# Two of 128 row tiles per history position fetched by SyncE, one DMA per row, instead of by GpSimd gathers

## The chip, the cores and the metric

The kernel runs on one NeuronCore of a Trainium2 chip. The metric is the device time of one execution in microseconds; the median of several executions is given. The engines are called by the names of the profile: PE (TensorE), DVE (VectorE), ACT (ScalarE), POOL (GpSimd) and SP (SyncE). SP computes nothing: it issues DMAs.

## The reference

It is the deep-interest network of a recommender, in float32, for a batch B of 16384 and L = 200 history positions, with embeddings of D = 64 numbers and a table of V = 100000 items. Cut to what matters:

```python
it = i_emb[item]                       # [B, 64]
h = i_emb[hist]                        # [200, B, 64]: 3,276,800 rows of the table
feat = concat([h, it, h - it, h * it], axis=-1)
a = dice(feat @ au_W1 + au_b1, au_alpha, axis=1)   # 36 hidden units; moments over B for each l
w = a @ au_W2 + au_b2
cur = sum(w * h, axis=0)
z = concat([u_emb[user], it, c_emb[cate], cur], axis=-1)
# then two dense layers with dice, and a last dense layer: [B, outputs]
```

`dice(x, alpha)` is `x * (p + alpha * (1 - p))` with `p = sigmoid((x - mean) / sqrt(var + eps))`. The indices of hist are random over the whole table.

## The kernel before, in words

**Preparation.** A table in HBM is built first, with 128 numbers (512 bytes) a row: the item's embedding and, behind it, the part of the hidden layer that depends on that embedding alone. So one fetched row brings both. The tensor `xi` in HBM holds the part that depends on `it` alone.

**Tiling.** The batch is cut into NT = 128 tiles of P = 128 rows. TD = 16 tiles make one chunk of 2048 rows, and there are ND = 8 chunks. A step k is one chunk of one position: l = k // 8, c = k % 8; there are 1600 steps. The loop `For_i` (L381) unrolls LPB = 10 positions, 80 steps, and runs 20 times; at the end of each pass all engines meet at a barrier.

**One step** (L344) does, with a software pipeline over k:
- `fetch(k)` (L295): POOL issues 16 indirect DMAs (`gather`, L138; the instruction has line L141), each of 128 rows of 512 bytes, by one column of `idx`, into `land[k % 4]`; SP loads `xi[c]` into `xit[k % 2]` (L298).
- ACT copies `xit` of k-1 into PSUM `px` (L353).
- DVE accumulates for k-11: `pw` times the embedding (L357), added to `curT` (L360).
- `turn(k-1)` (L300): DVE transposes the landed rows into `hx[(k-1) % 10]`, in four instructions, each of 64 partitions by 1024 elements (L306). ACT copies the embedding half into PSUM `pg` (L367).
- `hidden(k-2)` (L315): DVE adds `px` to the hidden half (L319) and takes its moments (L321). `product(k-1)` (L310): DVE multiplies by the item (L312), and PE adds the product's matmul to `px` (L179).
- For k-10 ACT and DVE apply the dice gate (L364, L374, L375), and PE multiplies by the second weight into `pw` (L179).

**Order.** Each engine works through its own queue in the order in which the code names the instructions (`manual_schedule`). At the first step of each l, ahead of everything else of the step, `load_hist_ids` (L151, the DMA has line L152) loads the indices of l+1 into `idx[(l+1) % 2]`; the same buffer served l-1, so SP holds that load until the last gather of l-1 has landed. SP holds the load of `xit` of step k until ACT has copied the one of step k-2, which ACT does in its step k-1. POOL holds the first gather of step k until the turn of step k-4 has freed `land`. Waits on SP's DMAs use eight semaphores in turn, so a DMA of SP waits for the one eight before it. POOL's gathers do likewise.

Of the kernel before, what the change touches and what calls it, by code (L numbers as in the profile page):

```python
# [8 lines left out]
F32 = mybir.dt.float32  # L9
I32 = mybir.dt.int32  # L10
# [4 lines left out]
P = 128  # L15
D = 64
EPS = 1e-8
CH = 512
S = 32
CD = 2 * CH  # L20
LPB = 10
LAND = 4
IDX = 2
XI = 2
RING = 10


@with_exitstack
def din_kernel(
# [24 lines left out]
    nc = tc.nc  # L54
    L, B = r_hist.shape
    NT = B // P
    TD = 2 * CD // P
    ND = NT // TD
    V = i_emb.shape[0]
# [3 lines left out]
    const = ctx.enter_context(tc.tile_pool(name="const", bufs=1))  # L63
# [7 lines left out]
    def quarter(e, g, n=S):  # L71

        return slice((2 * e + g) * S, (2 * e + g) * S + n)
# [21 lines left out]
    for e in range(2):  # L95
        rows = au_W1.rearrange("(g d) a -> d g a", d=D)[e * S : (e + 1) * S]
        for g in range(2):
            r = quarter(e, g)
            nc.sync.dma_start(au_w[r], rows)
            for q, (a0, n) in enumerate(parts):  # L100
                c, a = quarter(q, g, n), slice(a0, a0 + n)
# [6 lines left out]
    for g in range(2):  # L108
        for q, (a0, n) in enumerate(parts):
            r, a = quarter(q, g, n), slice(a0, a0 + n)  # L110
# [12 lines left out]

    land = [const.tile([P, TD, 2 * D], F32, name=f"land{i}") for i in range(LAND)]
    idx = [const.tile([P, NT], I32, name=f"idx{i}") for i in range(IDX)]
    stats = [const.tile([P, 2 * ND, nc.vector.BN_STATS_DIM], F32, name=f"st{i}") for i in range(2)]
    rstds = [const.tile([P, 1], F32, name=f"rs{i}") for i in range(2)]
    shifts = [const.tile([P, 1], F32, name=f"sh{i}") for i in range(2)]
# [5 lines left out]
    table = dram.tile([V, 2 * D], F32, name="table")  # L134
# [3 lines left out]
    def gather(dst, ids, rows):  # L138

        for n in range(ids.shape[1]):  # L140
            nc.gpsimd.indirect_dma_start(  # L141
                out=dst[:, n, :],
                out_offset=None,
                in_=rows,
                in_offset=bass.IndirectOffsetOnAxis(ap=ids[:, n : n + 1], axis=0),
            )
# [2 lines left out]
        nc.sync.dma_start(t, ids.rearrange("(p n) -> p n", n=NT))  # L149

    def load_hist_ids(i, l):  # L151
        nc.sync.dma_start(idx[i], r_hist[ds(l, 1), :].rearrange("l (p n) -> p (l n)", n=NT))  # L152

    def by_tile(t, i):

# [41 lines left out]
    with ExitStack() as start:  # L197
        pre = start.enter_context(tc.tile_pool(name="pre", bufs=3))
        ids = [start.enter_context(tc.tile_pool(name=f"ids{i}", bufs=1)).tile(
            [P, NT], I32, name=f"ids{i}") for i in range(3)]  # L200
        for t, v in zip(ids, (r_item, r_user, r_cate)):
            load_ids(t, v)
        load_hist_ids(0, 0)

        per = V // P
# [69 lines left out]
    with ExitStack() as main:  # L275
        ring = main.enter_context(tc.tile_pool(name="ring", bufs=1))
        hx = [ring.tile([P, 2, CD], F32, name=f"hx{i}") for i in range(RING)]
        xit = [ring.tile([P, CD], F32, name=f"xit{i}") for i in range(XI)]
        hm = ring.tile([P, CD], F32, name="hm")
        gate = ring.tile([P, CD], F32, name="gate")  # L280


        for t in hx + [pw, land[-1 % LAND]]:
            nc.vector.memset(t, 0.0)

        for t in px:
            layer(t, [(blk_m, hx[0][:, 0])])
        for i in range(2):
            for c in range(2 * ND):
                nc.vector.bn_stats(stats[i][:, c, :], hx[0][:, 0, :CH])  # L290
            nc.vector.memset(rstds[i], 0.0)
            nc.vector.memset(shifts[i], 0.0)
        nc.sync.dma_start(xit[-1 % XI], xi[ND - 1])

        def fetch(k):  # L295
            l, c = divmod(k, ND)
            gather(land[k % LAND], idx[l % IDX][:, ts(c, TD)], table)
            nc.sync.dma_start(xit[k % XI], xi[c])  # L298

        def turn(k):  # L300

            rows = land[k % LAND].rearrange("p n (s e c) -> p n s e c", s=2, e=2)
            for i in range(2):
                for e in range(2):
                    dst = hx[k % RING][ts(e, D), :, ts(i, CH)]
                    nc.vector.transpose(  # L306
                        dst.rearrange("p s (n t) -> p n s t", t=S), rows[ts(i, D), :, :, e]
                    )

        def product(k):  # L310

            nc.vector.tensor_mul(hm, pg, itT[:, k % ND])  # L312
            layer(px[k % 2], [(blk_m, hm)], onto=True)

        def hidden(k):  # L315

            l, c = divmod(k, ND)
            x = hx[k % RING][:, 1]
            nc.vector.tensor_add(x, px[k % 2], x)  # L319
            for i in range(2):  # L320
                nc.vector.bn_stats(stats[l % 2][:, 2 * c + i, :], x[:, ts(i, CH)])  # L321

        def moments(l):

            i = l % 2
            mv = small.tile([P, 2], F32, tag="mv", name="mv")
            nc.vector.bn_aggr(mv, stats[i].rearrange("p c s -> p (c s)"))
            other = small.tile([P, 2], F32, tag="other", name="other")
            for q in range(2):
                for g in range(2):  # L330
                    nc.vector.tensor_copy(other[quarter(q, g)], mv[quarter(q, 1 - g)])  # L331
            total = small.tile([P, 2], F32, tag="total", name="total")
            nc.vector.tensor_add(total, mv, other)
            mean = small.tile([P, 1], F32, tag="mean", name="mean")
            nc.vector.tensor_scalar_mul(mean, total[:, 0:1], 0.5)
            dev = small.tile([P, 1], F32, tag="dev", name="dev")
            nc.vector.tensor_sub(dev, mv[:, 0:1], mean)
            half = small.tile([P, 1], F32, tag="half", name="half")
            nc.vector.tensor_scalar_mul(half, total[:, 1:2], 0.5)
            var = small.tile([P, 1], F32, tag="var", name="var")  # L340
            nc.vector.scalar_tensor_tensor(var, dev, dev, half, ALU.mult, ALU.add)  # L341
            scale_and_shift(mean, var, P, rstds[i], shifts[i])

        def step(k, first=None, last=None):  # L344


            def has(j):
                return (first is None or j >= first) and (last is None or j <= last)

            if has(k):  # L350
                fetch(k)
            if has(k - 1):
                nc.scalar.copy(px[(k - 1) % 2], xit[(k - 1) % XI])  # L353
            if has(k - 11):

                j = k - 11
                nc.vector.scalar_tensor_tensor(  # L357
                    pw, pw, au_bias2, hx[j % RING][:, 0], ALU.add, ALU.mult
                )
                nc.vector.tensor_add(curT[:, j % ND], pw, curT[:, j % ND])  # L360
            if has(k - 10):
                j = k - 10
                i, x = j // ND % 2, hx[j % RING][:, 1]
                nc.scalar.activation(gate, x, AF.Sigmoid, bias=shifts[i], scale=rstds[i])  # L364
            if has(k - 1):
                turn(k - 1)
                nc.scalar.copy(pg, hx[(k - 1) % RING][:, 0])  # L367
            if has(k - 2):
                hidden(k - 2)
            if has(k - 1):  # L370
                product(k - 1)
            if has(k - 10):

                nc.scalar.activation(pg, gate, AF.Identity, bias=au_al, scale=au_1al)  # L374
                nc.vector.tensor_mul(x, pg, x)  # L375
                layer(pw, [(w2_rep, x)])
            if has(k - 2) and (k - 2) % ND == ND - 1:
                moments((k - 2) // ND)

        steps = LPB * ND  # L380
        with tc.For_i(0, L, LPB) as l0:  # L381
            with tc.manual_schedule():
                for k in range(steps):
                    if k % ND == 0:
                        l = k // ND + 1
                        load_hist_ids(l % IDX, (l0 + l) if l < LPB else (l0 + l) % L)
                    step(k)
        with tc.manual_schedule():
            for k in range(steps, steps + 11):
                step(k, first=0, last=steps - 1)  # L390


    with ExitStack() as head:
# [5 lines left out]
        for g in range(2):  # L399
            t = fin.tile([P, 4, Z1], F32, name=f"w1{g}")  # L400
            nc.vector.memset(t, 0.0)
            for e in range(2):
                rows = W1.rearrange("(f d) z -> d f z", d=D)[e * S : (e + 1) * S]
# [13 lines left out]
        for i, (v, n) in enumerate(((alpha1, Z1), (alpha2, Z2))):  # L417
            t = fin.tile([n, 1], F32, name=f"al{i}")
# [17 lines left out]
        for c in range(ND):  # L436
            rows = land[c % LAND].rearrange("p (s n) d -> p s (n d)", s=2)
# [20 lines left out]
        for m in range(2 * ND):  # L458
            a = work.tile([Z1, CD], F32, tag="a1", name="a1")
# [6 lines left out]
        for c in range(ND):  # L466
            a = work.tile([Z2, TD, 2, 2, S], F32, tag="a2", name="a2")
            for g in range(2):
                p, zm = (
                    t.rearrange("z (i n t) -> z i n t", i=2, t=S)  # L470
                    for t in dice(1, Z2, 2 * c + g, rstd, shift)
                )
# [38 lines left out]
```

## Time and profile before

| | us |
|---|---|
| median of 3 runs | 36814.77 (36811.52 to 36815.77) |
| the profiled execution | 32902.92 |
| its span, first to last instruction | 32901.1 |
| POOL, DVE, PE, ACT busy | 24515.6, 20753.5, 9945.4, 7691.1 |
| gathers of the loop (L141) | 25600, 943 ns each |
| transposes of the loop (L306) | 6404, 1239 ns each |
| first gather of the loop starts at | 489.46 |

The runs take 11.9% longer than the profiled execution; within each kind, the numbers agree closely. The profile's spans, waits and durations are all of the profiled execution. A group's row gives its line in the code, the engine, the operation, what it writes and reads, the count, the busy time, the mean duration of one in ns, and the idle time of the engine just before these instructions with what ended most of it; "issue" means that the engine waited for nothing that the profile shows. SPq is the queue of SP.

### The profile page before, as it was taken

Reading aid. Unit: us, or ns where it says so; the run is one execution under the profiler, and the core shown is the slowest. Engines: PE = TensorE matmul, PEld = TensorE weight load, DVE = VectorE, ACT = ScalarE, POOL = GpSimd, SP = SyncE. Lnnn points to the kernel's source line nnn. Section 1 sums busy time; section 2 is a strip of 40 time slices with the busy share of each in tenths; the row PEclk is TensorE's granted clock in tenths of the full one; section 3 lists DMA queues with packets and bytes.
Section 4 is the critical chain, followed back from the end, with each engine's and each line's share of the span. In section 5 each row is a group of like instructions: output and inputs, shape, how many; then the busy total and the mean of one; then the engine's idle time right before and its main releaser. Section 6 shows DMA issues by size and latency. Waiting matters only on the chain. (4 is left out here: it accounts for less than half of the span.)

```text
span 32901.1 us, 97527 instructions
## 1 busy us (share of the span) xinstructions
PE 9945.4 (30%) x13656; PEld 3845.6 (12%) x13656; DVE 20753.5 (63%) x20780; ACT 7691.1 (23%) x7146; POOL 24515.6 (75%) x25988
## 2 busy tenths in 40 slices
PE   3222222222222222222222222222322222222234
PEld 1111111111111111111111111111111111111112
DVE  7666666666666666666666666666666666666665
ACT  1222222222222222222222222222222222222222
POOL 7777777777777777777777777777777777777774
PEclk6666666666666666666666666666666666666666
DMA  5222222222222222222222222222222222222221
GB/s 158 79 79 80 79 79 78 79 80 79 79 79 79 79 78 81 78 80 79 79 79 79 80 79 79 79 79 79 79 78 81 79 79 79 79 79 79 80 79 53
DMA packets 1208018, 2647.92 MB, mean 80 GB/s; under 512 B 549094, under 2 KB 575366, under 8 KB 1201286
## 3 DMA queue, kind: packets, MB, share of 16 engines
q0 software_dynamic: 831488, 1691.97, 19.6%
q1 hardware_dynamic: 365382, 887.25, 8.7%
q10 hardware_dynamic: 10560, 63.79, 0.5%
q14 instruction: 576, 4.72, 0.0%
q8 instruction: 12, 0.20, 0.0%
HBM read 2577.30 MB, written 63.91 MB: 80 GB/s over the span
## 5 line engine op out<-in xcount | busy, mean ns | idle before, releaser
L141 POOL DMA_INDIRECT land<-table,idx x25600 | 24153.0, 943 | 7882.1 <-issue 7715.6
L179 PE MATMUL px<-hm,blk_m 128*128 128x512 f32 x6404 | 5971.8, 1088 | 22551.3 <-DVE hm L312 22551.3
L306 DVE STREAM_TRANSPOSE hx<-land 64x1024 f32<-64x1024 f32 x6404 | 7936.4, 1239 | 4282.0 <-DMA land<-table,idx 4217.2
L367 ACT COPY pg<-hx 128x1024 f32<-128x1024 f32 x1601 | 1627.5, 1017 | 19460.1 <-DVE hx L306 19460.1
L357 DVE SCALAR_TENSOR_TENSOR pw<-pw,au_bias,hx 128x1024 f32<-128x1024 f32 x1611 | 2082.6, 1293 | 5223.7 <-PE pw L179 5009.3
L179 PEld LDWEIGHTS px<-hm,blk_m 128*128 128x128 f32 x6404 | 1879.6, 324 | 25581.8 <-DVE hm L312 23927.8
L179 PE MATMUL pw<-hx,w_rep 128*128 128x512 f32 x6440 | 3869.3, 732 | 37.1 <-DVE hx L375 37.1
L375 DVE TENSOR_TENSOR hx<-pg,hx 128x1024 f32<-128x1024 f32 x1610 | 1971.8, 1225 | 2044.2 <-ACT pg L374 2044.2
L374 ACT ACTIVATE pg<-gate,au_al,au_1al 128x1024 f32<-128x1024 f32 x1610 | 1943.5, 1207 | 4330.1 <-DVE hm L312 4299.7
L179 PEld LDWEIGHTS pw<-hx,w_rep 128*128 128x128 f32 x6440 | 1800.6, 280 | 2851.0 <-issue 1973.4
L321 DVE BATCH_NORM_STATS2 st<-hx 128x6 f32<-128x512 f32 x3204 | 2061.1, 685 | 55.1
L360 DVE TENSOR_TENSOR curT<-pw,curT 128x1024 f32<-128x1024 f32 x1611 | 1972.6, 1224 | 54.9
L319 DVE TENSOR_TENSOR hx<-px,hx 128x1024 f32<-128x1024 f32 x1602 | 1962.0, 1225 | 49.5
L364 ACT ACTIVATE gate<-hx,sh,rs 128x1024 f32<-128x1024 f32 x1610 | 1991.9, 1237 | 3.1
L312 DVE TENSOR_TENSOR hm<-pg,itT 128x1024 f32<-128x1024 f32 x1601 | 1931.6, 1206 | 0.0
L353 ACT COPY px<-xit 128x1024 f32<-128x1024 f32 x1601 | 1594.8, 996 | 1.9 <-PE px L179 1.7
L364 ACT ACT_TABLE_LOAD x222 | 284.8, 1283 | 4.5 <-DVE sh L193 0.5
L188 ACT ACT_TABLE_LOAD x203 | 260.4, 1283 | 3.8
L179 PE MATMUL px<-rT,blk_h 128*128 128x512 f32 (+1 forms) x196 | 163.9, 978 | 226.2 <-DVE rT L162 226.2
L188 ACT ACTIVATE std<-var,eps 128x1 f32<-128x1 f32 x201 | 59.2, 295 | 456.0 <-DVE var L341 456.0
L331 DVE COPY other<-mv 32x2 f32<-32x2 f32 x804 | 155.2, 193 | 15.1
L353 ACT ACT_TABLE_LOAD x21 | 26.9, 1283 | 567.0 <-DMA idx<-in_r_hist 321.1
(74 smaller groups left out, 1754.0 us busy)
## 6 DMA issues: line engine op xcount, KB each, us to landing
xit<-xi SPq DMA_DIRECT2D x1601, 512.0 KB, 3.7
land<-table,idx POOLq DMA_INDIRECT x25600
table<-tab ACTq DMA_DIRECT2D x48, 1024.0 KB, 4.2
tab<-in_L_rec_i_emb SPq DMA_DIRECT2D x48, 512.0 KB, 4.4
idx<-in_r_hist SPq DMA_DIRECT2D x201, 64.0 KB, 1.8
ucT<-t ACTq DMA_DIRECT2D x16, 512.0 KB, 2.7
land<-ucT SPq DMA_DIRECT2D x16, 512.0 KB, 4.2
xi<-t ACTq DMA_DIRECT2D x8, 512.0 KB, 2.9
```

What stands on the lines that cost most here:

```text
L141: nc.gpsimd.indirect_dma_start(out=dst[:, n, :], out_offset=None, in_=rows, in_offset=bass.IndirectOffsetOnAxis(ap=ids[:, n : n + 1], axis=0),
L179: nc.tensor.matmul(dst[:, cols], lhsT, rhs[:, cols], start=(j == 0 and not onto), stop=(j == len(pairs) - 1), skip_group_check=onto,)
L306: nc.vector.transpose(dst.rearrange("p s (n t) -> p n s t", t=S), rows[ts(i, D), :, :, e])
L312: nc.vector.tensor_mul(hm, pg, itT[:, k % ND])
L319: nc.vector.tensor_add(x, px[k % 2], x)
L321: nc.vector.bn_stats(stats[l % 2][:, 2 * c + i, :], x[:, ts(i, CH)])
L357: nc.vector.scalar_tensor_tensor(pw, pw, au_bias2, hx[j % RING][:, 0], ALU.add, ALU.mult)
L360: nc.vector.tensor_add(curT[:, j % ND], pw, curT[:, j % ND])
L364: nc.scalar.activation(gate, x, AF.Sigmoid, bias=shifts[i], scale=rstds[i])
L367: nc.scalar.copy(pg, hx[(k - 1) % RING][:, 0])
L374: nc.scalar.activation(pg, gate, AF.Identity, bias=au_al, scale=au_1al)
L375: nc.vector.tensor_mul(x, pg, x)
```

## The change

In each l, two of the 128 tiles, the last of chunk 3 and the last of chunk 7, are no longer gathered by POOL. SP fetches their 256 rows, each with a DMA of its own from a byte address that it holds in a register, into one of four tiles `side` of [128, 128]. Each step issues 32 such rows, a quarter of a tile, behind its load of `xit`; they belong to the tile that is turned four to seven steps later. The addresses come from a second load per l of the indices concerned, into `addr` (256 numbers in one partition), which DVE multiplies by 512, the bytes of a row; one instruction of SP then loads 32 of them into 32 registers. The first tile's 128 rows are fetched ahead of the loop. The turn of chunk 3 and of chunk 7 becomes eight transposes: four of 64 x 960 from `land`, four of 64 x 64 from `side`.

```diff
+NS = 2
+SIDE = 4
+ROW = 4 * 2 * D
+    side = [const.tile([P, 2 * D], F32, name=f"side{i}") for i in range(SIDE)]
+    addr = [const.tile([1, NS * P], I32, name=f"addr{i}") for i in range(IDX)]
...
     def load_hist_ids(i, l):
-        nc.sync.dma_start(idx[i], r_hist[ds(l, 1), :].rearrange("l (p n) -> p (l n)", n=NT))
+        ids = r_hist[ds(l, 1), :]
+        nc.sync.dma_start(idx[i], ids.rearrange("l (p n) -> p (l n)", n=NT))
+        t = addr[i]
+        with nc.allow_non_contiguous_dma(reason="one index of each partition"):
+            nc.sync.dma_start(
+                t.rearrange("o (c p) -> o c p", c=NS),
+                ids.rearrange("l (p c n) -> l c n p", c=NS, p=P)[:, :, NT // NS - 1],
+            )
+        nc.vector.tensor_scalar_mul(t, t, ROW)
+
+    def has_side(k):
+        return (k + 1) % (ND // NS) == 0
...
+        flat = table.rearrange("v d -> (v d)").bitcast(U8)
+
+        def rows_by_address(m, part, of):
+
+            l, c = divmod(m, NS)
+            dst = side[m % SIDE].bitcast(U8)
+            n = P // of
+            _, at = nc.values_load_multi_w_load_instructions(
+                addr[l % IDX][:, c * P + part * n : c * P + (part + 1) * n],
+                engines=(mybir.EngineType.SP,), min_val=0, max_val=ROW * (V - 1),
+                skip_runtime_bounds_check_because="the DMA checks the address against the table",
+            )
+            for j, a in enumerate(at):
+                p = part * n + j
+                nc.sync.dma_start(dst[p : p + 1], flat[ds(a, ROW)].rearrange("(o d) -> o d", o=1))
 
         def fetch(k):
             l, c = divmod(k, ND)
-            gather(land[k % LAND], idx[l % IDX][:, ts(c, TD)], table)
+            n = TD - has_side(k)
+            gather(land[k % LAND][:, :n], idx[l % IDX][:, c * TD : c * TD + n], table)
             nc.sync.dma_start(xit[k % XI], xi[c])
+            m, part = divmod(k, ND // NS)
+            rows_by_address(m + 1, part, ND // NS)
 
         def turn(k):
 
-            rows = land[k % LAND].rearrange("p n (s e c) -> p n s e c", s=2, e=2)
-            for i in range(2):
-                for e in range(2):
-                    dst = hx[k % RING][ts(e, D), :, ts(i, CH)]
-                    nc.vector.transpose(
-                        dst.rearrange("p s (n t) -> p n s t", t=S), rows[ts(i, D), :, :, e]
-                    )
+            n = TD - has_side(k)
+            tiles = [(slice(0, n), land[k % LAND][:, :n])]
+            if has_side(k):
+                tiles.append((slice(n, TD), side[k // (ND // NS) % SIDE].unsqueeze(1)))
+            for at, rows in tiles:
+                rows = rows.rearrange("p n (s e c) -> p n s e c", s=2, e=2)
+                for i in range(2):
+                    for e in range(2):
+                        dst = hx[k % RING][ts(e, D), :, ts(i, CH)]
+                        nc.vector.transpose(
+                            dst.rearrange("p s (n t) -> p n s t", t=S)[:, at],
+                            rows[ts(i, D), :, :, e],
+                        )
...
+        for part in range(ND // NS):
+            rows_by_address(0, part, ND // NS)
         steps = LPB * ND
         with tc.For_i(0, L, LPB) as l0:
```

More of the change, by code (lines that the diff above doesn't have):

```diff
@@ L25 @@
 RING = 10
+NS = 2
+SIDE = 4
+ROW = 4 * 2 * D
+U8 = mybir.dt.uint8
 @with_exitstack
@@ L284, in din_kernel @@
             nc.vector.memset(t, 0.0)
+        for t in side:
+            nc.vector.memset(t, 0.0)
         for t in px:
```

## The prediction

> **What bounds the kernel now.** I read the busy line of the page, the costliest groups, the timeline of one step in mid-loop, the waits of SyncE's queue, then the instructions of single lines. First the page's busy line and three groups (line, engine, operation, count, busy us, mean ns, idle before and its releaser):
>
> ```profile
> PE 9945.4 (30%) x13656; PEld 3845.6 (12%) x13656; DVE 20753.5 (63%) x20780; ACT 7691.1 (23%) x7146; POOL 24515.6 (75%) x25988
> L141 POOL DMA_INDIRECT land<-table,idx x25600 | 24153.0, 943 | 7882.1 <-issue 7715.6
> L306 DVE STREAM_TRANSPOSE hx<-land 64x1024 f32<-64x1024 f32 x6404 | 7936.4, 1239 | 4282.0 <-DMA land<-table,idx 4217.2
> xit<-xi SPq DMA_DIRECT2D x1601, 512.0 KB, 3.7
> ```
>
> POOL is 75% busy, yet it is the bound: of its 7882 us of idle time before gathers, 7716 are "issue", time in which it waited for nothing. Gathers follow each other at a fixed pitch; DVE is what waits, 4217 us in all for rows to land. The timeline of one step (start, us, engine, operation, idle before):
>
> ```profile
> 15070.12 0.95 POOL L141 DMA_INDIRECT land<-table,idx  x1 [0.30 <-issue]
> 15070.17 5.00 DVE L306 STREAM_TRANSPOSE hx<-land 64x1024 f32<-64x1024 f32 x4 [2.87 <-DMA land<-table,idx]
> 15070.19 0.34 SPq L152 DMA_DIRECT2D idx<-in_r_hist  x1
> ...
> 15090.09 0.94 POOL L141 DMA_INDIRECT land<-table,idx  x1 [0.30 <-issue]
> 15090.30 5.00 DVE L306 STREAM_TRANSPOSE hx<-land 64x1024 f32<-64x1024 f32 x4 [2.83 <-DMA land<-table,idx]
> ```
>
> Sixteen gathers lie between the two POOL rows: 19.97 us, 1.248 us each (0.94 of work, 0.30 of issue). 25600 of these are 31959 us of the 32901 us span. DVE's idle time ahead of its transposes, 2.7 us a step (4217/1563), is its whole slack: every other idle stretch of its step is a dependence on PE or ACT. SP now does two things a step, and mostly waits; its queue's waits (us, times, longest), and its DMA instructions (duration ns min/median/max):
>
> ```profile
> SPq L298 <- ACT px L353: 20885.5, 1222, 45.0
> SPq L152 <- DMA land<-table,idx: 8655.8, 720, 45.1
> L152 SPq DMA_DIRECT2D idx<-in_r_hist x201: 342/343/430, 9.2 to 32366.2; - x101
> L298 SPq DMA_DIRECT2D xit<-xi x1600: 319/320/596, 498.3 to 32476.9; - x178
> DMA to landing us min/median/max: 1.7/1.8/2.0
> 4.03 0.42 SPq L113 DMA_DIRECT2D au_w<-in_L_rec_au_W  x1
> 4.49 0.37 SPq L111 DMA_DIRECT2D au_bias<-in_L_rec_au_b  x1
> 4.90 0.25 SPq L112 DMA_DIRECT2D au_al<-in_L_rec_au_alpha  x1
> 5.20 0.30 SPq L113 DMA_DIRECT2D au_w<-in_L_rec_au_W  x1
> ```
>
> The load of idx has its address in a register and holds SP for 0.343 us; back to back at the program's start, a DMA takes 0.25 to 0.43 us with 0.04 to 0.05 between two. The landing row is that of idx.
>
> [...] both queues together hold the DMA engines for 28% of the span (19.6 and 8.7), so issuing time is the thing to save. [...]
>
> **The change, part by part.** The timed runs (median 36814.77) lie 11.9% above the profiled execution (32902.92, its span and 1.8 us around it). No view says why. The sums are made against 32902.92 and carried over by ratio; if the whole excess sits in the 25984 gathers, each costs 0.151 us more there, 1.40 us, which gives nearly the same.
>
> (a) Removed: two of 128 gathers per l, 400 in all, on the engine that sets the end: 400 x 1.248 = 499 us less.
>
> (b) Added on SP, in every step: one register load of 32 words and 32 row DMAs, between two xit loads. A row at the idx row's 0.343 plus 0.045 is 0.39; 32 are 12.5 us (9.6 at 0.25+0.05, 15.4 at 0.43+0.05). The register load is in no view. [...] I take 4.0, an estimate[...]. With the xit load (0.42) a step of SP is 16.9 us, between 10.6 and 22.2. SP is further held at the idx load of each l until the gathers of the l before have landed (the 8656 us above), so it cannot bank time across an l: it needs 8 x 16.9 + 1.5 for idx and addr + 2.5 for the landing = 139 us, while POOL takes 126 x 1.248 = 157.3. Hidden, with 18 us to spare; it decides from 19.2 us a step ((157.3 - 4)/8). Behind SP's rows stands the next xit load: ACT's copy into px waits for that, and through PE and DVE all else does.
>
> (c) Waits of the rows. In the built program each DMA of SP waits for the one eight before it to land. At 1.8 us (the idx load) eight in flight allow one per 0.23 us; this is nothing until a row takes 8 x 0.39 = 3.1 us. The xit load's 3.7 us is covered, since a register load and seven rows follow it.
>
> (d) addr on DVE. Once per l DVE gets the multiply by 512 (1 x 256, 0.15 to 0.35 us; the 128x1 multiplies take 0.147 to 0.154) at the head of step 8l, where it waits for the addr load. That DMA stands behind the idx load, so behind the same landing that releases the turn; I estimate it lands 4 to 12 us later (idx took 1.8; 256 small descriptors add to it). Queued behind the multiply are the two accumulations and then the turn, so the turn is late by 7 to 15 us. POOL notices only when the turn of step k-4 is missing, about three steps or 53 us of cover; DVE wins back 2.3 us a step (2.7 less the 0.3 by which POOL's mean step shrinks), 18 us per l. Cost: nothing, and at a loop boundary nothing either, as DVE is idle there for 14.3 us.
>
> (e) Turns. A side step has eight transposes for four. The 64x512 form takes 0.71 and the 64x1024 form 1.24, so 0.18 fixed and 1.04 ns an element: 4 x (1.18 + 0.25 - 1.24) = 0.8 us, 1.6 per l, within the same slack.
>
> (f) Start. Before the loop SP fetches the first 128 rows. It gets going at about 497 us, needs 124 x 0.39 + 3 x 4 = 60, and only then issues idx, addr and xit of step 0. DVE, held by the first addr, does its first turn near 590, while POOL wants that buffer after 63 gathers, 489.5 + 78.6 = 568. A stall of some 23 us, once[...].
>
> Sum: 32902.9 - 499 + 23 = 32427, 0.9855 of before. On the timed runs 36815 x 0.9855 = 36281; I take 36,285. If the excess over the profile is not in the gathers, 36815 - 476 = 36,340; own range 36,230 to 36,420.
>
> **Rivals.** *SP becomes the bound.* One mechanism: a row DMA plus its share of the register load costs more than 0.59 us ((19.2 - 0.42)/32; about 0.66 if POOL's pitch is 1.40 in the timed runs). [...] Against it: 0.343 us in the trace for a DMA with an address in a register. At the upper ends (22.2 us a step) an l takes 8 x 22.2 + 4 = 181.6, the loop 36320 against 32036, and the whole, with 164 us of loop boundaries, 37,374; if SP is slower in the timed runs as POOL may be, more. I give 37,400.
>
> *DVE becomes the bound through addr.* If the 256 descriptors land late enough (turn late by more than about 18 us), DVE no longer catches up within an l, and the rest is paid 200 times: at 30 us late 200 x 12 = 2400 less the 499, some 38,700. Against it: the idx load of 64 KB lands in 1.8 us.
>
> *No difference.* In the timed runs something other than POOL sets the pace (the excess of 11.9% is unexplained), with room for (b) and (d): 36,815. Against it: no engine but POOL is within 2 us of its step in the profile.
>
> That the rows are not where the diff puts them is excluded: the built program has 32 row DMAs after each xit load and 126 gathers per l.
>
> **How the numbers follow.** Forecast 0.60; SP bound 0.26; DVE bound 0.08; no difference 0.06. What a measurement of this kernel can tell from no change is about 0.2%, 74 us. Faster 0.60, same 0.06, slower 0.34. Low end 36,200: 400 gathers at 1.40 are 560 us, no start stall, and little beyond. The high end must take in most of the SP case, from its 37,374 part of the way to the same scaled by 1.119 (41,800): 38,400 leaves out about 0.12 above.
>
> **What would show it.** Right: 25200 gathers at 0.94 with 0.30 of issue before them; SP waiting for ACT's px copy in most steps; the gap before the gathers at one place near 568 us only; the multiply waiting for addr once per l, and turns back on their landing before the l ends. Wrong: gathers idle for DVE's turn throughout, ACT's px copy waiting for the xit DMA, a register load near or above 6 us, row DMAs above 0.43 us or with waits between them; or turns waiting for the multiply in every step.

## The result, and the profile after

The changed kernel took 45896.81 us (median of 4 runs, 45853.32 to 45938.01), the kernel before beside it 36813.14 (4 runs, 36807.65 to 36815.77): 1.2468 times as long, interval 1.2446 to 1.2489. The forecast was 36285.

That is half of the result. The experiments ran in six batches, each with the kernel before beside it. In the first batch it took 36839 us, as in the runs above; in the five later ones it took 32901 to 32903 us, the time of the profiled execution that the forecast was worked from (32902.92). There the same changed kernel took 32514.80 us (4 runs, 32513.69 to 32515.51): 0.9882 of before, interval 0.9866 to 0.9899, faster by 387 us. The two settings are called S (before 36.8 ms) and F (before 32.9 ms) below. Nothing in this study chooses between them, and what they are is not known: the batches were put on chips with several numbers, and one number occurs in both. So there are two profiles after.

First setting S. The page of the changed kernel: the busy line, and the rows that answer to those shown of before (line, engine, operation, count | busy us, mean ns | idle before and its releaser).

```profile
PE 9890.8 (22%) x13656; PEld 3823.3 (8%) x13656; DVE 21020.5 (46%) x22589; ACT 7686.2 (17%) x7146; POOL 24137.3 (53%) x25588
L148 POOL DMA_INDIRECT land<-table,idx x25200 | 23774.7, 943 | 21182.4 <-DVE hx L349 12331.0
L349 DVE STREAM_TRANSPOSE hx<-land 64x1024 f32<-64x1024 f32 (+1 forms) x6404 | 7813.7, 1220 | 106.5 <-DMA land<-table,idx 36.6
L397 ACT COPY px<-xit 128x1024 f32<-128x1024 f32 x1601 | 1620.5, 1012 | 26407.9 <-DMA xit<-xi 25251.3
L167 DVE TENSOR_SCALAR addr<-addr 1x256 int32<-1x256 int32 x201 | 57.7, 287 | 5471.7 <-DMA addr<-in_r_hist 5471.7
```

POOL is busy for 53% of the span and waits 12331 us for DVE's turns. ACT waits 25251 us for the `xit` load, a row that the forecast named as the mark of being wrong. In the profile of before, the same copy waited for 2 us in all:

```profile
L353 ACT COPY px<-xit 128x1024 f32<-128x1024 f32 x1601 | 1594.8, 996 | 1.9 <-PE px L179 1.7
```

`xit` stands behind the rows in SP's queue, and SP itself waits for almost nothing; among its waits (us, times, longest) the largest at the line of the rows is

```profile
SPq L328 <- DMA side<-table: 355.7, 545, 1.9
```

The trace of S lacks many semaphore records (it holds 167,944 updates, that of F 569,179), so a view of waits can miss some; the starts and durations of all 51,328 row DMAs are in it. SP's instructions at the row line and at the register load (count: ns min/median/max, first and last start in us):

```profile
L328 SPq MOVE side<-table x51328: 1/29/1413, 594.0 to 45560.5; - x200
L328 SPq DMA_DIRECT2D side<-table x51328: 1/228/1419, 594.1 to 45560.6; - x200
L321 SPq TENSOR_LOAD <-addr x1604: 2/2057/3800, 576.3 to 45548.3; - x179
```

So SP is the bound. From one idx load to the next is 224.5 us in the mean, 28.1 us a step, and 200 of these are 44,900 of the 45,936 us span. The medians are below what was forecast; it is the maxima that count. SP's timeline shows when (start, us, count):

```profile
20020.20 35.70 SPq L328 DMA_DIRECT2D side<-table  x14
20058.00 0.70 SPq L334 DMA_DIRECT2D xit<-xi  x1
20064.31 17.54 SPq L328 DMA_DIRECT2D side<-table  x32
...
20107.13 20.32 SPq L328 DMA_DIRECT2D side<-table  x32
20128.26 0.00 SPq L334 DMA_DIRECT2D xit<-xi  x1
20130.13 25.18 SPq L328 DMA_DIRECT2D side<-table  x32
...
20181.03 10.68 SPq L328 DMA_DIRECT2D side<-table  x32
```

The same 32 rows take 10.7 us or 25, and once the last 14 of a step take 36. In the slow stretches a MOVE is as slow as a row DMA, in the mean 1.12 us from its start to the next. Sorted by how long POOL has been gathering without a stop (stops over 1 us), or has been stopped, the mean time from the start of such an instruction to that of SP's next one is, worked out from the trace of 5 to 45 ms:

```
ns                      MOVE   row DMA
POOL gathering  < 4 us    85      277
               4-12 us   246      353
                >12 us  1119     1122
POOL stopped    < 3 us   549      512
               3-10 us   176      331
                >10 us    67      270
```

A row (one MOVE, one DMA) costs 0.34 us beside a POOL that stopped a while ago and 2.24 us late in a run of gathers. (The 0.36 and 2.28 of an expectation below count SP's other DMAs and its waits in.) Half of the rows go out while POOL is stopped, a third in the first 12 us of a run of gathers; the remaining 18% take 18 of the 40 ms. POOL in turn stops because SP is late: it waits the 12331 us for DVE's turns, which come behind the 25251 us that ACT waits for `xit`. The mean of the loop is 0.77 us a row.

Now setting F. The same rows of the changed kernel's page there:

```profile
PE 9909.3 (30%) x13656; PEld 3837.2 (12%) x13656; DVE 21024.2 (65%) x22589; ACT 7692.9 (24%) x7146; POOL 24139.3 (74%) x25588
L148 POOL DMA_INDIRECT land<-table,idx x25200 | 23776.7, 944 | 7872.6 <-issue 7536.4
L349 DVE STREAM_TRANSPOSE hx<-land 64x1024 f32<-64x1024 f32 (+1 forms) x6404 | 7823.1, 1222 | 2004.7 <-DMA land<-table,idx 1936.7
L167 DVE TENSOR_SCALAR addr<-addr 1x256 int32<-1x256 int32 x201 | 68.8, 342 | 2454.7 <-DMA addr<-in_r_hist 2454.7
L397 ACT COPY px<-xit 128x1024 f32<-128x1024 f32 x1601 | 1595.6, 997 | 5.2 <-PE px L197 3.9
```

POOL is the bound as before, and its idle time is "issue" again. ACT's copy waits 5 us in all. SP's waits, its instructions, and its timeline there:

```profile
SPq L160 <- DMA land<-table,idx: 6109.8, 419, 34.6
SPq L334 <- ACT px L397: 3018.6, 605, 7.5
```

```profile
L321 SPq TENSOR_LOAD <-addr x1604: 2023/2062/3908, 462.2 to 32092.9; - x179
L328 SPq MOVE side<-table x51328: 29/29/38, 480.2 to 32105.1; - x200
L328 SPq DMA_DIRECT2D side<-table x51328: 224/228/407, 480.3 to 32105.1; - x200
```

```profile
20118.90 0.90 SPq L334 DMA_DIRECT2D xit<-xi  x1
20122.09 10.32 SPq L328 DMA_DIRECT2D side<-table  x32
20132.50 0.36 SPq L334 DMA_DIRECT2D xit<-xi  x1
20135.07 10.73 SPq L328 DMA_DIRECT2D side<-table  x32
```

No MOVE is longer than 38 ns. A step of SP, from one `xit` load to the next, takes 13.0 to 13.6 us where it doesn't wait, and SP waits for ACT and for landings of gathers, not ACT for it.

### The profile page after: what moved, and what is told of

It is laid out like the page before. It is cut to its first block, busy times and chain, and to the rows that moved or that the text cites. A ratio compares the mean times of both kernels' runs of the same rounds, so it can differ in the third digit from the quotient of the medians.

```text
span 45936.2 us, 207379 instructions
## 1 busy us (share of the span) xinstructions
PE 9890.8 (22%) x13656; PEld 3823.3 (8%) x13656; DVE 21020.5 (46%) x22589; ACT 7686.2 (17%) x7146; POOL 24137.3 (53%) x25588
## 3 DMA queue, kind: packets, MB, share of 16 engines
q0 software_dynamic: 818688, 1665.73, 13.9%
## 5 line engine op out<-in xcount | busy, mean ns | idle before, releaser
L148 POOL DMA_INDIRECT land<-table,idx x25200 | 23774.7, 943 | 21182.4 <-DVE hx L349 12331.0
L349 DVE STREAM_TRANSPOSE hx<-land 64x1024 f32<-64x1024 f32 (+1 forms) x6404 | 7813.7, 1220 | 106.5 <-DMA land<-table,idx 36.6
L167 DVE TENSOR_SCALAR addr<-addr 1x256 int32<-1x256 int32 x201 | 57.7, 287 | 5471.7 <-DMA addr<-in_r_hist 5471.7
L349 DVE STREAM_TRANSPOSE hx<-side 64x64 f32<-64x64 f32 x1604 | 383.9, 239 | 35.0
L188 DVE STREAM_TRANSPOSE tab<-px 64x512 f32<-64x512 f32 (+1 forms) x196 | 139.6, 712 | 138.6 <-issue 96.8
```

The costliest lines, as they stand in the source:

```text
L148: nc.gpsimd.indirect_dma_start(out=dst[:, n, :], out_offset=None, in_=rows, in_offset=bass.IndirectOffsetOnAxis(ap=ids[:, n : n + 1], axis=0),
L349: nc.vector.transpose(dst.rearrange("p s (n t) -> p n s t", t=S)[:, at], rows[ts(i, D), :, :, e],)
```

## The experiments

The first batch met setting S, all later ones F. Theory A, after the first profile: SP's instructions slow down while POOL gathers. B: rows and register loads are too dear by themselves. C: the addr load holds SP. In the diffs `-` and `+` are against the changed kernel where nothing else is said.

**1. The kernel before again** (`b_again`, no edit), for a second profile of it.

> The kernel before, unchanged, profiled beside the others. If the profile of before was taken under other conditions than its timed runs, this one spans about 36,810 us and shows where the 3,910 us lie: longer gathers (1.40 us a gather), or idle time of POOL. If the profiler itself makes the difference, it spans 32,900 again and nothing of the excess can be seen.

36838.59 us against 36839.44, ratio 1.0 (0.999 to 1.0009). Its page holds the other half of the puzzle:

```profile
L141 POOL DMA_INDIRECT land<-table,idx x25600 | 26449.6, 1033 | 9454.1 <-issue 8588.3
L357 DVE SCALAR_TENSOR_TENSOR pw<-pw,au_bias,hx 128x1024 f32<-128x1024 f32 x1611 | 2082.8, 1293 | 13185.9 <-remote 10157.2
L306 DVE STREAM_TRANSPOSE hx<-land 64x1024 f32<-64x1024 f32 x6404 | 7922.0, 1237 | 296.4 <-DMA land<-table,idx 227.0
```

In the profile of before, gathers took 943 ns and DVE waited 4282 us at its turns. Here gathers take 1033 ns and follow each other at 1.40 us, both in the mean ((26449.6 + 9454.1)/25600; the median pitch is 1.254), and DVE no longer waits for landings but 13186 us ahead of L357, for PE's result in `pw`. In the first profile of before that wait was

```profile
L357 DVE SCALAR_TENSOR_TENSOR pw<-pw,au_bias,hx 128x1024 f32<-128x1024 f32 x1611 | 2082.6, 1293 | 5223.7 <-PE pw L179 5009.3
```

So the 11.9% between that profile and the timed runs was a difference of setting. Not every step between engines is slower in S. Worked out from the two traces, DVE to PE, DVE to ACT and ACT to DVE take the same 0.03 to 0.06 us in both, in the median; but from the end of PE's last matmul into `pw`, as the profile models that end, to DVE's start on it is 0.04 us in the first profile and 5.2 here. One step in S:

```profile
20024.00 2.81 PE L179 MATMUL pw<-hx,w_rep 128*128 128x512 f32 x4
20031.62 1.29 DVE L357 SCALAR_TENSOR_TENSOR pw<-pw,au_bias,hx 128x1024 f32<-128x1024 f32 x1 [8.74 <-remote]
```

**2. The POOL half alone.** No rows, no register loads, no addr; the side tiles stay zero.

```diff
-            nc.sync.dma_start(
-                t.rearrange("o (c p) -> o c p", c=NS),
-                ids.rearrange("l (p c n) -> l c n p", c=NS, p=P)[:, :, NT // NS - 1],
-            )
-        nc.vector.tensor_scalar_mul(t, t, ROW)
...
-            rows_by_address(m + 1, part, ND // NS)
...
-            rows_by_address(0, part, ND // NS)
```

> The half of the change on POOL alone: 126 gathers per l, the side tiles left at zero, no row DMAs, no register loads, no addr (two tiles per l of the result are left out). If POOL's gathers set the pace in the timed runs as in the profile: 36,813 less 400 x 1.25 to 1.40, so 36,250 to 36,315. If something else sets the pace there: 36,813.

> The kernel of pool_part (126 gathers per l; no rows, register loads or addr, so the side tiles stay zero). Where the kernel before takes 32.9 ms: the forecast says that all that SP and DVE are given to do costs no more than the 23 us of its start stall, so 32490 to 32515 us, and the changed kernel's 32515 lies 0 to 25 us above it. If the 100 us lost at the pass ends come from SP's longer program: 32400 to 32430 us. Where it takes 36.8 ms: 36410 us again.

In S 36409.66 us, 0.9883 of before (0.9866 to 0.9899), 430 us less. In F 32498.95, 0.9877 (0.9861 to 0.9894), 403 less. So the loss in S is wholly in what SP and DVE were given, and in F all of that together costs 16 us (32515 less 32499). The page in F:

```profile
L148 POOL DMA_INDIRECT land<-table,idx x25200 | 23776.3, 944 | 7858.5 <-issue 7709.1
L340 DVE STREAM_TRANSPOSE hx<-land 64x1024 f32<-64x1024 f32 (+1 forms) x6404 | 7829.5, 1223 | 3506.9 <-DMA land<-table,idx 3442.2
```

**3. No gathers in the loop**: nothing but the 256 rows per l is fetched.

```diff
-        for t in hx + [pw, land[-1 % LAND]]:
+        for t in hx + [pw] + land:
...
-            gather(land[k % LAND][:, :n], idx[l % IDX][:, c * TD : c * TD + n], table)
```

> The changed kernel without the loop's gathers (the rows of land stay zero, so the result leaves them out); SP's rows, register loads and addr as in the change. Theory A (SP's instructions slow down while POOL gathers): a row takes its undisturbed 0.32 us throughout, SP needs 13 us a step, and DVE sets the pace at 17 to 18 us a step, 28,000 to 30,000 us in all. Theory B (SP's rows and register loads are too dear by themselves): SP keeps its 28 us a step, about 45,500 us. Theory C (the addr load alone holds SP, some 80 us per l): 200 x (13 x 8 + 80) = 36,800 and 870 more, about 37,700 us.

> The kernel of no_gathers (the gathers of the loop are left out, so nothing but the 256 rows per l is fetched), which took 28452 us on the chip where the kernel before takes 36.8 ms. Theory A3 (the two kinds of chip differ only in what runs beside gathers): where the kernel before takes 32.9 ms it takes the same, 28350 to 28550 us. Rival (the chip of the first runs is slower in everything): 25400 to 27500 us.

28452.58 us in S (0.7723 of before, 0.7708 to 0.7739), 28360.88 in F (0.862, 0.8606 to 0.8634). SP's row line in S, beside a POOL that does nothing in the loop:

```profile
L328 SPq MOVE side<-table x51328: 29/29/38, 590.5 to 28059.2; - x200
L328 SPq DMA_DIRECT2D side<-table x51328: 224/228/432, 590.6 to 28059.2; - x200
```

All 51328 rows at the pace of setting F; this settles A against B. In F these rows run from 480.0 to 27961.7 us. From the first row to the last it is thus 27469 us in S and 27482 in F, equal to 0.05%. The rows start 110 us later in S; so the 92 us between the medians lie ahead of the loop, where POOL gathers too. The two settings differ beside gathers and nowhere else that this kernel shows. With the gathers go their packets (818,688 in the queue `software_dynamic` of the changed kernel, 12,288 here) and, in F, most semaphore updates (14.4 per us in the kernel before, 5.67 here); this run takes all of them away together.

**4. addr loaded once**, ahead of the loop (later rows are those of the first positions).

```diff
-    def load_hist_ids(i, l):
+    def load_hist_ids(i, l, first=False):
...
+        if not first:
+            return
         t = addr[i]
...
-        load_hist_ids(0, 0)
+        load_hist_ids(1, 1, True)
+        load_hist_ids(0, 0, True)
```

> The changed kernel with addr loaded ahead of the loop alone, so the 256 rows of an l are those of l = 0 or 1 (the result leaves the right rows of these tiles out); the rows, register loads and gathers are all there. Theory C: the slow stretch of some 80 us at the head of each l goes, 200 x 70 us are won, and POOL bounds again, 36,300 to 37,500 us. Theory A: the slow stretches stay wherever gathers run, 42,000 to 45,500 us. Theory B: 45,500 us.

> The kernel of addr_once (addr is loaded and multiplied only ahead of the loop, so the rows fetched later are those of the first positions), which took 47302 us on the chip where the kernel before takes 36.8 ms. Where the kernel before takes 32.9 ms: DVE's wait for addr, 2455 us in the changed kernel, is gone, and DVE waits that much longer for its rows to land instead: 32500 to 32520 us, no gain. If that wait did cost time in spite of DVE's slack: up to 100 us less.

In S 47301.7 us (2 runs), 1.284 of before (1.2802 to 1.2877): no gain, so C falls. (It is 1405 us longer than the changed kernel; why, stays open.) The wait of ACT's copy is still there:

```profile
L400 ACT COPY px<-xit 128x1024 f32<-128x1024 f32 x1601 | 1626.3, 1016 | 31016.3 <-DMA xit<-xi 30064.6
```

In F 32506.56 us, 0.988 (0.9863 to 0.9896), 8 us under the changed kernel. Those 8 are one stall of POOL's gathers near the start (8.4 us in the changed kernel's trace, none in this one's). The 2455 us that DVE waits for addr cost nothing else.

**5. Half the rows** (16 of 32 in each step; the others are left out):

```diff
-            n = P // of
+            n = P // of // 2
...
```

> Each step fetches 16 of its 32 rows by SP; the other half of each side tile stays zero (64 of 256 rows per l from each tile are left out), POOL still does 126 gathers per l. In the changed kernel's profile a row (MOVE and DMA) takes 0.36 us of SP when POOL has not gathered for 10 us, and 2.28 us from 12 us into an unbroken run of gathers; the mean over everything is 0.77. Theory A1 (SP's instructions slow down only after POOL has gathered back to back for about 10 us, and recover some 3 to 10 us after it stops): with half the rows SP still needs POOL to pause in every step, so 38500 to 42000 us, and POOL's gathers stay in runs of about 16 with gaps between. Theory A2 (a row costs 0.77 us whenever there are gathers about): a step of SP is 16 x 0.77 + 2.0 + 0.4 = 14.7 us, less than POOL's 22, so SP is hidden again and the time is that of the POOL half alone, 36300 to 36700 us.

> The kernel of half_rows again (16 of the 32 rows of each step are left out), beside the changed kernel on one chip. Where the kernel before takes 32.9 ms: 32504 us again, 1.2% faster, and the changed kernel within 0.3% of it (theory A3) or far above it (theory A1). Where the kernel before takes 36.8 ms: 38500 to 42000 us if SP's rate depends on how long POOL has gathered without a stop, 36300 to 36700 if a row costs 0.77 us throughout.

> The kernel of half_rows once more (16 of the 32 rows of each step are left out), for a chip on which the kernel before takes 36.8 ms: 38500 to 42000 us if SP's rate there depends on how long POOL has gathered without a stop (0.36 us a row at first, 2.28 us a row after 12 us), 36300 to 36700 us if a row costs 0.77 us throughout. Where the kernel before takes 32.9 ms: 32504 us again.

> The kernel of half_rows (16 of the 32 rows of each step are left out), for a chip on which the kernel before takes 36.8 ms: 38500 to 42000 us if SP's rate there depends on how long POOL has gathered without a stop, 36300 to 36700 us if a row costs 0.77 us throughout. Where the kernel before takes 32.9 ms: 32504 us again.

32503.86 us, 0.9878 of before (0.9862 to 0.9895); in three later batches 32503.26, 32503.21 and 32503.66. All four met F. What they show: doubling the rows, from 16 to 32 a step, costs 11 us of 32,500, so SP is off the path. What they were made for, the number of rows that SP can carry in S, stays open.

**6. Rows from fixed addresses** (no addr, register load or MOVE; not the rows of the indices):

```diff
...
-            for j, a in enumerate(at):
+            for j in range(n):
+                a = ROW * ((part * n + j) * 733 + 97 * c)
```

> The 32 row DMAs of each step stay, but from addresses fixed in the program: no load of addr, no multiply, no register load and no MOVE (the rows fetched are not those of the indices). SP issues 33 instructions a step in place of 66. Theory B (what is dear is addressing by registers: the register load and the MOVEs): SP's step is 32 x 0.27 + 0.4 = 9 us, hidden, 36300 to 36700 us. Theory A1 (every SP instruction, of whatever kind, slows to about 1.15 us once POOL has gathered back to back for 10 us): the 33 instructions take 9 us at the fast pace and the pace holds for about 8 to 10 us of a run of gathers, so POOL still has to pause in many steps: 37000 to 41500 us, and the profile again shows row DMAs 1.1 to 1.2 us apart in the later part of a run of gathers.

> The kernel of fixed_rows (rows from fixed addresses, so not those of the indices; 33 instructions of SP a step in place of 66), for a chip on which the kernel before takes 36.8 ms: 37000 to 41500 us if each instruction of SP slows to 1.15 us beside dense gathers; 36300 to 36700 us if the register load and the MOVEs are what is slow. Where the kernel before takes 32.9 ms: 32504 us again.

32504.16 and 32503.12 us (both 0.9879, 0.9862 to 0.9895), in F again. Addr, register loads and MOVEs together cost 11 us there, the stall of experiment 4 among them; in S it stays open.

**7. A pause on POOL after each gather**, in the changed kernel and, with the same edit, in the kernel before:

```diff
+    rest_t = const.tile([P, 64], F32, name="rest_t")
...
-            gather(land[k % LAND][:, :n], idx[l % IDX][:, c * TD : c * TD + n], table)
+            for j in range(n):
+                gather(land[k % LAND][:, j : j + 1], idx[l % IDX][:, c * TD + j : c * TD + j + 1], table)
+                nc.gpsimd.memset(rest_t, 0.0)
```

> The changed kernel with one short memset (128 x 64) on POOL after each gather of the loop, so that gathers follow each other at some 1.5 us in place of 1.25; nothing is left out. Theory A1 in the form that it is the density of gathers that starves SP: SP's instructions stay near 0.36 us a row, SP's step near 14 us, POOL becomes the bound again at 126 x its new pitch: 200 x 126 x 1.5 = 37800 plus 700, 37500 to 40500 us, faster than the changed kernel by 12 to 18%. Theory A2 (any overlap with gathers costs SP the same) and a theory that only a real stop of POOL frees SP: the time stays at 44500 to 48500 us.

> The kernel of paced (a short memset on POOL after each gather; nothing left out), for a chip on which the kernel before takes 36.8 ms: 37500 to 41000 us if a pause between gathers frees SP, 44500 to 48500 us if only a stop of POOL does[...]. Where the kernel before takes 32.9 ms: 33439 us again.

> The kernel before with one short memset (128 x 64) on POOL after each gather of the loop, as in paced; nothing is left out. Where the kernel before takes 32.9 ms, gathers go from a pitch of 1.249 to 1.280 us as in paced: 25600 x 0.031 = 800 us more, 33600 to 33800 us. Where it takes 36.8 ms, gathers are 1.40 us apart there: theory A1 (a density of gathers slows the other engines and, through these, POOL): a slightly lower density helps at least a little, 35500 to 36700 us; a theory that the chip is slower whatever POOL does: 37300 to 37800 us.

33438.91 and 33438.45 us (1.0163 of before, 1.0146 to 1.018), and 33832.08 for the kernel before with the pause (1.0283, 1.0266 to 1.03), all in F.

```profile
L149 POOL DMA_INDIRECT land<-table,idx x25200 | 23962.3, 951 | 4419.2 <-issue 4389.5
L336 POOL MEMSET rest_t<- 128x64 f32 x25200 | 4231.6, 168 | 16.0
```

Most of the memset (168 ns) fits into the 0.30 us of issue between gathers: the median pitch rises from 1.249 to 1.280, not to the 1.5 that I had reckoned. With some longer ones the mean within a pass goes from 1.2488 to 1.2853 us, and 25200 x 0.0365 = 920 us are the 924 measured. Every 0.01 us on a gather is 250 us: POOL is the bound, in both kernels. Whether a pause frees SP in S stays open.

**8. The changed kernel again**:

> The changed kernel unaltered, to see whether its time goes with the pace at which the chip at hand runs the kernel before. In the last three runs the kernel before took 32903 us, and SP's instructions were nowhere slowed (a row some 0.36 to 0.4 us of SP, also late in a run of gathers); in the four runs ahead of these it took 36839 us, and SP's instructions took 1.15 us each once POOL had gathered for 10 us. Theory A3 (one thing slows both: on a chip where the kernel before takes 36.8 ms, SP starves beside the gathers and the changed kernel takes 44.5 to 47.5 ms; on one where it takes 32.9 ms it does not, and the changed kernel takes 32430 to 32560 us, 1.0 to 1.4% faster). Theory A1 (SP starves beside dense gathers on any chip, and half_rows and paced escaped because they have fewer instructions or a pause): above 38000 us on any chip.

32514.80 us, as told above. Theory A3 holds, with nothing changed in the code: where the kernel before takes 32.9 ms, SP does not starve and the change gains 1.2%. For S, the changed kernel itself has the runs of the result alone; there `addr_once`, in another batch, shows the same.

**9. Twenty positions in the loop body**, so 10 passes in place of 20:

```diff
-LPB = 10
+LPB = 20
```

> The changed kernel with 20 positions unrolled in the loop body in place of 10, so 10 passes in place of 20; nothing is left out. In the profile of the changed kernel on a chip where SP is not slowed, POOL's gathers stop for 9.5 us more than their pitch at each of 19 pass ends (4.2 us in the kernel before), 180 us in all, which is what the forecast's sum (32427) lacks against 32515. Theory (the stop is paid once per pass): 9 stops in place of 19, 90 to 100 us less, 32410 to 32430 us where the kernel before takes 32.9 ms. Rival (the stop grows with the length of the pass[...]): 32500 to 32600 us. Where the kernel before takes 36.8 ms: 44500 to 47500 us, as the changed kernel.

32411.68 us (4 runs), 0.9851 of before (0.9835 to 0.9867), in F; it beats both kernels. In the changed kernel POOL's gathers stop for 180.0 us beyond their pitch at the 19 ends of passes, here for 74.7 at 9. The difference, 105 us, is the 103 us gained. In setting S this version was not run, and the kernel before with 20 positions in neither; so these 103 us are no gain of the change as such.

## Why the prediction was wrong, and where it was right

**(a), the gathers.** 400 x 1.248 = 499 us was right for the pitch in F, which stays at 1.249, but the POOL half alone saves 403 us there (430 in S). The forecast's sum for the profiled setting, 32427, missed 32515 by 88 us, because of a term that no step had. At the end of a pass POOL's gathers stop for 9.6 us beyond their pitch instead of 4.0 (the first end apart); 19 ends make 180 us for 80. It comes with the 126 gathers alone: `pool_part_c`, without any of the new work, has the same 178 us. POOL's DRAIN at the pass end ends 7.75 us after the last gather there, in place of 1.9; no run shows why.

**(b), SP's step: the step that failed.** It was forecast at 16.9 us, at most 22.2, and hidden below 19.2; in the timed runs, in S, it took 28.1 and set the time. The prices of the DMAs were taken from instructions of an SP that had little to do, in setting F; the register load's 4.0 us, and its share of the 22.2, were an estimate that no trace of before showed. In F the step was put too high: a row is 0.323 us from start to start when nothing disturbs it (0.39 forecast), the register load 2.06 us for 32 registers, 0.064 each (4.0 for all). A step is some 13.3 us for the 16.9 forecast, and hidden. What failed is that the step was carried to the timed runs, where 11.9% were unexplained, by a ratio, as though every duration there scaled alike. SP's did not: 28.1 us a step, 2.1 times the undisturbed step, where the mean pitch of the gathers, in the kernel before, rose by 12% (1.40 for 1.25). In such a setting the change gives the new work to an engine that is slowed beside the very instructions whose number it cuts by 1.6%.

**(c), eight DMAs in flight.** Right: SP's DMAs use eight semaphores in turn in the trace of the changed kernel in S (6668 to 6689 DMAs each), and 50,602 of the 51,328 row DMAs wait on the one that they use themselves, so for the DMA eight before. In F the view of SP's waits has none for a row to land, and in S they are 356 us in all, 1.9 at the longest.

**(d), addr.** Right in F: DVE waits 12.4 us for it each time (2454.7/198), where a turn 7 to 15 us late was forecast, and its slack swallows that: its waits for landings fall from 3442 (`pool_part_c`) to 1937 us. In S the wait is 27 us (5471.7 over 200 loads), and `addr_once` shows that it is not the cause. A load of addr is 258 packets under 512 bytes where 256 descriptors were forecast: `addr_once_c`, with 199 fewer of these loads, has 51,326 fewer such packets.

**(e), turns.** The 64x64 transposes take 239 ns (0.25 forecast) and the 64x960 ones 1171 ns (1180): right, and hidden.

**(f), the start.** 8.4 us of stall against 23 forecast, as rows and register loads were cheaper: 124 x 0.323 + 4 x 2.1 = 48 us in place of 60. The place was wrong: POOL stopped at 549 us, after 48 gathers, not near 568 after 63. The first step of the loop also turns the step before it, whose buffer is the one that the fourth step's gathers need.

**The rivals.** "SP becomes the bound" named the place, and the marks (ACT's copy waiting for the `xit` load, 25251 us). Its threshold, 0.59 to 0.66 us a row, fits: the mean row is 0.77 in S and 0.323 in F. Its price does not: 37,374, or 41,800 scaled, because it let the register load decide, by the estimate above, and gave no row more than 0.48 us. A row's data is one packet of 512 bytes: these packets in the queue of SP's DMAs rise from 26,112 to 77,440, by 51,328, one a row. "DVE becomes the bound through addr" and "no difference" fall.

**The open gap.** A profile 11.9% under the runs it stands for was taken as unexplained and scaled away. The profile that was needed was of the setting of the timed runs; `b_again` shows there what the first one could not: DVE waits 8.2 us a step ahead of L357 (13186/1611) in place of 3.2, behind PE's last matmul, and no instruction that the profile shows accounts for it.

## What to carry to other kernels

If the profiled execution and the timed runs differ by more than their scatter, find out what differs before anything is scaled: get a profile whose span is that of the timed runs, and see which waits have grown. Time an alteration more than once in separate batches, beside the kernel before; here the one edit is 25% slower or 1.2% faster, and both agree within themselves to 0.2%. A price taken from a nearly idle queue holds for work beside the engine that dominates the kernel only if a trace shows it there (a row was 0.34 us beside a POOL that had stopped, and 2.24 late in a run of gathers): ask for the maxima, not the medians.

## What the runs showed of the hardware that was not expected

- In setting S, from about 12 us into an unbroken run of gathers, SP's MOVEs and row DMAs both come at 1.12 us each in the mean; more than 10 us after POOL has stopped they are back at 0.067 (MOVE) and 0.270 (row DMA). In F they are at 0.063 and 0.269 late in a run of gathers.
- The slow ones do not follow the gathers (1.249). Of their intervals, 89% lie within 0.04 us of 0.70, 1.40 or 2.10 us (28, 53 and 8%), and in half of the MOVEs the instruction lasts 0.70 us and the next one starts another 0.70 later. Two more numbers of the kernel before in S come to 0.70: its trace has 1.42 semaphore updates per us, one per 0.70; and from PE's first matmul of a step to DVE's L357 it is 11.19 us in the median (5.97 in F), a stretch that holds 8 matmuls and 8 weight loads, 0.70 for each of the 16. That the three have one cause is not shown.
- The transfers of the gathers do not back up in S: in the changed kernel's trace the last of a gather's sixteen packets of 4096 bytes, and of its sixteen of 4 bytes, ends 2.19 us after the gather's start, in the median, for the first gather of a run as for the hundredth. In the profile of before, in F, it is 2.19 too.
- The trace of S lacks most of its semaphore records while POOL gathers: the 1.42 updates per us of the kernel before are 14.4 in F; without gathers in the loop it is 5.67 in both. What the engines wait for in S, and whether the recording has a part in it, is not shown: no run separates recording from the kernel, and what makes a batch S or F stays open.
- A row DMA whose address is in a register holds SP for 0.228 us and its MOVE for 0.029.
